# Attention's scores of two groups of heads, with products on different rows of TensorE's array next to each other in its queue

## The chip, the cores and the metric

The kernel runs on one core of a Trainium2 chip. The core has five engines, each with a queue of its own that it works through in order: TensorE (PE; its weight loads are shown as PEld) multiplies matrices into PSUM, VectorE (DVE), ScalarE (ACT) and GpSimdE (POOL) work element by element, and SyncE (SP) issues transfers. The metric is the time of one launch in microseconds (us), the median over several runs.

## The reference

One decoder layer with three parts, each followed by a residual add and a layer norm, for 4 batches of 512 tokens with 512 features:

- attention inside windows of 128 tokens. The input is compressed to 256 features; there are 16 heads of 16 features. Per window and head: `scores = q @ k.T * scale + rel_bias[rel]`, `probs = softmax(scores)`, `ctx = probs @ v`, and the output projection back to 512 features;
- a state-space recurrence (512 channels, 16 states each) over the context, gated with the attention's output;
- a feed-forward with ternary weights (the signs of W_g, W_u and W_d, 2048 hidden features) on activations rounded to 8 bits.

The bias `rel_bias[rel]` is the same 128x128 matrix for every head and window.

## The kernel before

The work is written as threads: generators that emit instructions and yield a cost. `weave` (L885) draws from them in the order of planned times and sets a priority; the framework's scheduler, which keeps a time line of its own, then fixes the order of each engine's queue. An edit in one thread can so move the instructions of all others. On the chip the queues run in order, and semaphores tie them together. The threads are, per batch: the recurrence's inputs, its steps, attention's projections (`attn_qk`, L574), four attention windows (`attn_window`, L603; a window waits for the one two before it), and the gate. After all windows comes the feed-forward: `ffn_load` gives attention's memory back and loads the signs of W_d (`ffn_setup2`, L738, the tile sd), and eight half batches follow (`ffn`, L750).

PSUM has eight banks. Four of them form one ring, from which `bank(...)` (L107, L110) draws for scores, projections and feed-forward; the others belong to the recurrence (`da`, `y`) and to its inputs and gates.

An attention window takes its 16 heads in four groups of four. The transposed q and k lie so that the four heads of group g stand in the 32 rows from 32g on, in NM = 2 blocks of features. `scores(g)` (L622) draws a bank and does on TensorE: two products with the identity that put the bias into the bank (high and low part, L625, 128x512), and two products q.k on the rows of the group (L634), each for two heads and 256 columns. k is kept in two versions, one for each half of the 32 rows, with the other half zero, so that one product gives two heads. A `tile_position` of (32g, 0) names the group's 32 rows of the array. VectorE then takes the maximum per head (L642). The loop over groups calls `scores(g + 1)` before it works on group g: four exponentials on ScalarE (L658), four transposes into the same bank (L662), a copy (L664), and four products with v (L669). The window ends with transposes, the output projection (L701) and the residual add (L702).

A recurrence step (`ssm_steps`, L357) has two or three large products on GpSimdE (L390, L400), four exponentials on ScalarE (L394), four scans on VectorE (L396), two products (L398), and four products on TensorE that sum the states into y (L404), with `tile_position` (0, 32j). There are 64 such steps, four for each batch and block of 128 channels, and each block has an opener (L380). The gate (`ssm_gate`, L415) multiplies y into the gate (L433), transposes it (L436) and adds it (L438). The feed-forward has products for the gate (L778), for the other factor (L802) and down (L830).

Of the kernel before, what the change touches and what calls it, by code (L numbers as in the profile page):

```python
# [15 lines left out]
ALU = mybir.AluOpType  # L16
AX = mybir.AxisListType

P = 128
# [6 lines left out]
NM = HC // P  # L26
# [41 lines left out]
HP = 1000  # L68
# [12 lines left out]
def decoder_layer_kernel(  # L81
# [21 lines left out]
    nc = tc.nc  # L103
# [6 lines left out]
    def bank(name):  # L110
        return psum.tile([P, 512], F32, tag="mm", name=name)
# [8 lines left out]
    ident = keep.tile([P, P], F32, tag="ident", name="ident")  # L120
# [98 lines left out]
    for j in range(NQ):  # L219
# [5 lines left out]
            lhsT=spreads[j],  # L225
            rhs=col[:, C_AL : C_AL + NE * DS],
            start=True,
            stop=True,
# [374 lines left out]
    def attn_window(b, w, aw, ap, aq, ws):  # L603
        n = f"{b}_{w}"
        tok = ts(w, P)
        cT, qT, kT = attn_x[b]
        xs = ap.tile([P, H], F32, tag="xa", name=f"xa{n}")
        nc.sync.dma_start(out=xs, in_=x[b * S + w * P : b * S + (w + 1) * P, :])
        yield 4

        v1 = ws["v1"][w % 2]
        pv = bank(f"v_ps{n}")
        for c in range(NM):
            nc.tensor.matmul(pv[:, :HC], lhsT=cT[:, c, tok], rhs=ws["v"][:, c, :], start=(c == 0), stop=False)
        nc.tensor.matmul(pv[:, :HC], lhsT=ws["one"], rhs=ws["row"][:, :HC], start=False, stop=True)
        nc.scalar.copy(v1[:, :, :DH], pv[:, :HC].rearrange("p (h d) -> p h d", d=DH))
        yield 1
        ntop = small.tile([P, HEADS], F32, tag="ntop", name=f"ntop_{n}", bufs=2)
        NG4 = HEADS // 4
        pscs = {}  # L620

        def scores(g):  # L622
            psc = bank(f"sc_ps{n}_{g}")
            for i in range(2):
                nc.tensor.matmul(  # L625
                    psc,
                    lhsT=ws["ident"],
                    rhs=ws["bias"][i].unsqueeze(1).to_broadcast([P, 4, P]),
                    start=(i == 0),
                    stop=False,  # L630
                )
            rows_ = ts(g, 32)
            for m in range(NM):
                nc.tensor.matmul(  # L634
                    psc[:, ts(m, 2 * P)],
                    lhsT=qT[rows_, m, tok],
                    rhs=kT[rows_, m, :, tok],
                    start=False,
                    stop=(m == NM - 1),
                    tile_position=(32 * g, 0),  # L640
                )
            nc.vector.tensor_reduce(  # L642
                ntop[:, 4 * g : 4 * g + 4], psc.rearrange("p (h k) -> p h k", k=P), AX.X, ALU.max, negate=True
            )
            pscs[g] = psc

        scores(0)
        yield 1
        pa = None
        for g in range(NG4):  # L650
            if g + 1 < NG4:
                scores(g + 1)
                yield 1.5
            psc = pscs.pop(g)
            sc = ap.tile([P, 4, P], F32, tag="sc", name=f"sc_{n}_{g}")
            for j in range(4):
                h = 4 * g + j
                nc.scalar.activation(sc[:, j, :], psc[:, ts(j, P)], AF.Exp, bias=ntop[:, h : h + 1])  # L658

            pt = psc  # L660
            for j in range(4):
                nc.tensor.transpose(pt[:, ts(j, P)], sc[:, j, :], ident)  # L662
            scT = ap.tile([P, 4, P], F32, tag="scT", name=f"scT_{n}_{g}")
            nc.scalar.copy(scT.rearrange("p h k -> p (h k)"), pt)  # L664
            if pa is None:

                pa = bank(f"a_ps{n}")
            for j in range(4):
                nc.tensor.matmul(  # L669
                    pa[32 * j : 32 * j + 32, ts(g, P)],  # L670
                    lhsT=v1[:, 4 * g + j, :],
                    rhs=scT[:, j, :],
                    start=True,
                    stop=True,
                    tile_position=(0, 32 * j),
                )
            yield 2
        av = ap.tile([P, NG4, P], F32, tag="scT", name=f"av_{n}")
        nc.scalar.copy(av.rearrange("p g q -> p (g q)"), pa)

        pq = pa
        for g in range(NG4):
            nc.tensor.transpose(pq[:, ts(g, P)], av[:, g, :], ident)
        pq3 = pq.rearrange("p (h d) -> p h d", d=32)
        den = small.tile([P, HEADS, 1], F32, tag="den", name=f"den_{n}", bufs=2)
        nc.vector.reciprocal(den, pq3[:, :, DH : DH + 1])
        at = ap.tile([P, HC], F32, tag="at", name=f"at_{n}")
        nc.vector.tensor_tensor(
            at.rearrange("p (h d) -> p h d", d=DH), pq3[:, :, :DH], den.to_broadcast([P, HEADS, DH]), ALU.mult
        )  # L690
        yield 3
        pt = pa
        for c in range(NM):
            nc.tensor.transpose(pt[:, ts(c, P)], at[:, ts(c, P)], ident)
        aT = ap.tile([P, HC], F32, tag="at", name=f"aT_{n}")
        nc.scalar.copy(aT, pt[:, :HC])
        yield 2
        po = pa
        nc.tensor.matmul(po, lhsT=ws["one"], rhs=ws["row"][:, HC:], start=True, stop=False)
        for c in range(NM):  # L700
            nc.tensor.matmul(po, lhsT=aT[:, ts(c, P)], rhs=ws["d"][:, c, :], start=False, stop=(c == NM - 1))  # L701
        nc.vector.tensor_tensor(xs, xs, po, ALU.add)  # L702
        nc.sync.dma_start(out=x0d[b][:, w, :], in_=xs)
# [216 lines left out]
    for b in range(B):  # L920
        threads.append((TP[b], after([], ssm_inputs(b), f"inputs{b}"), OP))
        threads.append((T0[b], after([f"inputs{b}"], ssm_steps(b, DT[b]), f"steps{b}"), OS))
        threads.append((TG[b], after(attn[b * NT : (b + 1) * NT] + [f"gate{b - 1}"] * (b > 0), ssm_gate(b), f"gate{b}"), OG))
        threads.append((TA[b] - AQ, after(["biases"], attn_qk(b, *aps), f"qk{b}"), OA))
        for w in range(NT):
            k = b * NT + w
            needs = [f"qk{b}"] + attn[k - 2 : k - 1] if k > 1 else [f"qk{b}"]
            threads.append((TA[b] + w * AW, after(needs, attn_window(b, w, *aps), attn[k]), OA))
# [68 lines left out]
```

## Time and profile before

| What | us |
|---|---|
| median of 9 runs | 831.48 (825.98 to 845.48) |
| the profiled execution's own time | 832.68 |
| its span, from the first instruction to the last | 830.9 |
| TensorE busy | 758.7 (91%) |
| VectorE busy | 649.0 (78%) |
| ScalarE busy | 591.8 (71%) |
| GpSimdE busy | 557.6 (67%) |
| score products q.k (L634), busy on TensorE | 74.1 |
| bias products (L625), busy on TensorE | 34.0 and 25.7 |
| attention's last residual add ends at | 539.3 |
| the recurrence's last y product starts at | 678.3 |
| starts of the down products of the eight half batches | 548.3, 585.4, 637.6, 678.8, 711.8, 742.4, 771.6, 800.8 |

How to read the profile: a row of the groups names the line, the engine, the operation, the tiles written and read, the form and the count, then the busy time in us and the mean duration in ns, and then the idle time before these instructions and who ended it. A product of 32-bit values has two passes, so that it shows as two records. The mean duration of a product contains the time that it takes to run through the array, which overlaps with the next one; what a product costs the queue is read from one start to the next. In the rows of 40 slices a digit is a tenth of the slice (20.8 us) in which the engine was busy. The chain is the work that ended last, followed back from the end.

### The profile page before, as it was taken

The page shows a single profiled execution, that of the slowest core. Times are in us where ns is not written, and L with a number is a line of the kernel's source. Part 1 is how long each engine was busy: PE and PEld are TensorE (multiplying, and loading weights), DVE is VectorE, ACT ScalarE, POOL GpSimd, SP SyncE. Part 2 cuts the span into 40 slices and gives each one's busy share as a digit, 9 for nine tenths or more (in the row PEclk, how much of TensorE's full clock was granted, in tenths as well). Part 3 has the DMA queues.
Part 4 walks back from the last instruction along what each step waited for, and adds up shares of the span by engine and source line. Part 5 has one row for each costly group of instructions (what it writes and reads, how often), then busy time and mean ns, then how long its engine had stood idle before and what let it go on. Part 6 is the DMA issues. An engine that isn't in the chain of part 4 may idle for free.

```text
span 830.9 us, 11702 instructions
## 1 busy us (share of the span) xinstructions
PE 758.7 (91%) x3906; PEld 413.0 (50%) x3906; DVE 649.0 (78%) x943; ACT 591.8 (71%) x1038; POOL 557.6 (67%) x323
## 2 busy tenths in 40 slices
PE   9977799999899999999988998889788999999995
PEld 4323244444344444434444454546464667777773
DVE  4459586899899986989988888989998978553542
ACT  3568889786866867786787878687596776845551
POOL 2158489599758968878876886797889944233342
PEclk9998898999989989899999999999999999999998
DMA  7887688866242536646153276582334112301100
GB/s 214 302 267 223 216 266 307 301 221 210 88 140 84 166 110 208 218 143 225 58 176 114 92 248 235 168 333 58 128 109 145 52 40 102 91 24 51 52 26 26
DMA packets 82784, 129.49 MB, mean 156 GB/s; under 512 B 18690, under 2 KB 29074, under 8 KB 81444
## 3 DMA queue, kind: packets, MB, share of 16 engines
q1 hardware_dynamic: 65844, 108.77, 40.2%
q10 hardware_dynamic: 16880, 19.98, 7.0%
q8 instruction: 31, 0.51, 0.3%
q14 instruction: 29, 0.24, 0.1%
HBM read 91.48 MB, written 37.23 MB: 155 GB/s over the span
## 4 chain that ended last, share of the span: by engine, by line
PE 55%; DVE 17%; ACT 12%; DMA 7%; issue 5%; POOL 2%; SPq 1%; ACTq 0%; DVEq 0%; POOLq 0%
PE d_ps L830 10%; PE y L404 6%; PE sc_ps L634 5%; DVE da L396 4%; PE u_ps L802 4%; PE g_ps L778 4%; DVE state L396 3%; PE a_ps L701 3%; PE sc_ps L625 3%; PE c_ps L568 2%; PE in_ps L273 2%; ACT da L394 2%; PE sc_ps L662 2%; DMA sgd<-sgn_sgd 2%; DVE state L398 2%
## 5 line engine op out<-in xcount | busy, mean ns | idle before, releaser
L390 POOL TENSOR_TENSOR state<-du,bc 128x1024 f32<-128x1024 f32 x128 | 302.0, 2374 | 115.4 <-PE y L404 69.6
L394 ACT ACTIVATE da<-d,a_neg 128x512 f32<-128x512 f32 x256 | 174.9, 696 | 63.7 <-DVE state L398 38.6
L400 POOL TENSOR_TENSOR state<-state,bc 128x1024 f32<-128x1024 f32 x64 | 151.9, 2373 | 38.9 <-DVE state L396 24.4
L396 DVE TENSOR_TENSOR_SCAN state<-da,state 128x512 f32<-128x512 f32 x128 | 152.5, 1208 | 31.5 <-ACT da L394 19.9
L396 DVE TENSOR_TENSOR_SCAN da<-da,state 128x512 f32<-128x512 f32 x128 | 152.9, 1214 | 16.3 <-ACT da L394 16.3
L823 POOL TENSOR_TENSOR lo<-gs,hi 128x512 fp32r<-128x512 f32 x64 | 82.5, 1293 | 103.4 <-ACT hi L821 87.9
L404 PE MATMUL y<-state,sel 128*32 128x512 f32 x512 | 104.0, 659 | 7.5 <-DVE state L398 4.6
L398 DVE TENSOR_TENSOR state<-da,bc 128x512 f32<-128x512 f32 x128 | 84.7, 678 | 0.8
L658 ACT ACTIVATE sc<-sc_ps,ntop 128x128 f32<-128x128 f32 x256 | 74.0, 375 | 11.2 <-DVE ntop L642 10.4
L821 ACT CAST hi<-gs 128x512 fp32r<-128x512 f32 x64 | 39.1, 615 | 56.4 <-DVE gs L811 42.8
L830 PE MATMUL d_ps<-sd,hi 128*128 128x512 f32 x256 | 73.8, 408 | 5.3 <-DVE gs L786 2.0
L830 PE MATMUL d_ps<-sd,lo 128*128 128x512 f32 x256 | 75.6, 417 | 0.0
L634 PE MATMUL sc_ps<-k,q 32*128 32x256 f32 x256 | 74.1, 410 | 0.7 <-ACT q L590 0.7
L802 PE MATMUL u_ps<-taken,su 128*128 128x256 bf16 x512 | 67.6, 273 | 6.5 <-DVE gs L811 4.2
L778 PE MATMUL g_ps<-taken,sg 128*128 128x256 bf16 x512 | 67.6, 276 | 4.5 <-DVE gs L811 3.2
L811 DVE TENSOR_TENSOR gs<-gs,u_ps 128x512 f32<-128x512 f32 x64 | 43.5, 680 | 34.6 <-PE u_ps L802 34.5
L786 DVE TENSOR_TENSOR gs<-g_ps,taken 128x512 f32<-128x512 f32 x64 | 43.4, 683 | 31.6 <-PE g_ps L778 28.1
L802 PEld LDWEIGHTS <-su 128*128 128x128 fp8e4 x512 | 46.3, 98 | 30.7 <-issue 23.5
L778 PEld LDWEIGHTS <-sg 128*128 128x128 fp8e4 x512 | 46.9, 98 | 28.0 <-issue 22.4
L634 PEld LDWEIGHTS sc_ps<-k,q 32*128 32x128 f32 x256 | 42.6, 187 | 30.0 <-issue 24.0
L830 PEld LDWEIGHTS d_ps<-sd,hi 128*128 128x128 f32 x256 | 45.1, 189 | 18.5 <-ACT hi L821 3.1
L642 DVE TENSOR_REDUCE ntop<-sc_ps 128x4 f32<-128x512 f32 x64 | 43.3, 677 | 13.8 <-PE sc_ps L634 13.6
(161 smaller groups left out, 1191.4 us busy)
## 6 DMA issues: line engine op xcount, KB each, us to landing
d<-dd SPq DMA_DIRECT2D x60, 256.0 KB, 3.8
du<-dud SPq DMA_DIRECT2D x60, 256.0 KB, 4.6
bc<-bcd SPq DMA_DIRECT2D x32, 256.0 KB, 4.0
xT<-in_xT_dram SPq DMA_DIRECT2D x16, 256.0 KB, 4.7
xa<-in_x_dram SPq DMA_DIRECT2D x16, 256.0 KB, 3.6
raw_sgd<-in_wgT_dram SPq DMA_DIRECT2D x16, 256.0 KB, 4.5
ud<-u ACTq DMA_DIRECT2D x4, 1024.0 KB, 4.3
uq<-ud SPq DMA_DIRECT2D x16, 256.0 KB, 3.0
```

The source lines that it names most:

```text
L390: nc.gpsimd.tensor_tensor(st, du, bb.unsqueeze(1).to_broadcast([P, 2, S]), ALU.mult)
L394: nc.scalar.activation(da, d[:, j, :], AF.Exp, scale=a_neg[:, a : a + 1])
L396: nc.vector.tensor_tensor_scan(to, da, st[:, j, :], 0.0, ALU.mult, ALU.add)
L398: nc.vector.tensor_tensor(st[:, j, :], da, cb, ALU.mult)
L400: nc.gpsimd.tensor_tensor(st, st, cb.unsqueeze(1).to_broadcast([P, 2, S]), ALU.mult)
L404: nc.tensor.matmul(y[ts(j, EB), :], lhsT=sel, rhs=sts[j], start=False, stop=(n == NG - 1), tile_position=(0, EB * j))
L634: nc.tensor.matmul(psc[:, ts(m, 2 * P)], lhsT=qT[rows_, m, tok], rhs=kT[rows_, m, :, tok], start=False, stop=(m == NM - 1), tile_position= ...
L658: nc.scalar.activation(sc[:, j, :], psc[:, ts(j, P)], AF.Exp, bias=ntop[:, h : h + 1])
L778: nc.tensor.matmul(pg[:, ts(j, HS)], lhsT=sg[:, c, ts(2 * f2 + j, P)], rhs=qT[:, c, :], start=(c == 0), stop=(c == NC - 1),)
L802: nc.tensor.matmul(pu[:, ts(j, HS)], lhsT=su[:, c, ts(2 * f2 + j, P)], rhs=qT[:, c, :], start=(c == 0), stop=(c == NC - 1),)
L823: nc.gpsimd.tensor_tensor(lo, g2, hi.bitcast(F32), ALU.subtract)
L830: nc.tensor.matmul(pos[t], lhsT=part[:, j, ts(t, P)], rhs=sd[:, 2 * f2 + j, :], start=(f2 + j == 0 and part is parts[0]), stop=(f2 == NF2 ...
```

## The change

`scores` takes two groups at once, (0, 1) and then (2, 3). It first draws the two banks and issues the four bias products, then the four products q.k in the order block 0 of both groups, block 1 of both groups. These four are held back until the last bias product has been scheduled (`issue_after`) and get a higher priority, so that they stand next to each other in the queue. The two maxima follow. The loop no longer asks for the scores of group g + 1 ahead of the work on group g: it asks for a pair before groups 0 and 2. The planned costs per window change from 1 and three times 1.5 to twice 2.

```diff
-        def scores(g):
-            psc = bank(f"sc_ps{n}_{g}")
-            for i in range(2):
-                nc.tensor.matmul(
-                    psc,
...
-            rows_ = ts(g, 32)
-            for m in range(NM):
-                nc.tensor.matmul(
-                    psc[:, ts(m, 2 * P)],
-                    lhsT=qT[rows_, m, tok],
-                    rhs=kT[rows_, m, :, tok],
...
+        def scores(gs):
+
+            for g in gs:
+                pscs[g] = bank(f"sc_ps{n}_{g}")
+                for i in range(2):
+                    last_bias = nc.tensor.matmul(
+                        pscs[g],
...
+            with tc.issue_after(last_bias.ins), tc.high_priority(HP):
+                for m in range(NM):
+                    for g in gs:
+                        nc.tensor.matmul(
+                            pscs[g][:, ts(m, 2 * P)],
+                            lhsT=qT[ts(g, 32), m, tok],
+                            rhs=kT[ts(g, 32), m, :, tok],
+                            start=False,
+                            stop=(m == NM - 1),
+                            tile_position=(32 * g, 0),
+                        )
...
-        scores(0)
-        yield 1
+
         pa = None
         for g in range(NG4):
-            if g + 1 < NG4:
-                scores(g + 1)
-                yield 1.5
+            if g % 2 == 0:
+                scores((g, g + 1))
+                yield 2
             psc = pscs.pop(g)
```

More of the change, by code (lines that the diff above doesn't have):

```diff
@@ L620, in attn_window @@
         pscs = {}
-        def scores(g):
-            psc = bank(f"sc_ps{n}_{g}")
-            for i in range(2):
-                nc.tensor.matmul(
-                    psc,
[L627 to L630, printed above, removed]
-                )
-            rows_ = ts(g, 32)
-            for m in range(NM):
-                nc.tensor.matmul(
-                    psc[:, ts(m, 2 * P)],
-                    lhsT=qT[rows_, m, tok],
-                    rhs=kT[rows_, m, :, tok],
[L638 to L645, printed above, removed]
@@ L647, in attn_window @@
-        scores(0)
-        yield 1
+        def scores(gs):
[4 more added lines that the diff above has]
+                        pscs[g],
+                        lhsT=ws["ident"],
+                        rhs=ws["bias"][i].unsqueeze(1).to_broadcast([P, 4, P]),
+                        start=(i == 0),
+                        stop=False,
+                    )
[9 more added lines that the diff above has]
+                            tile_position=(32 * g, 0),
+                        )
+            for g in gs:
+                nc.vector.tensor_reduce(
+                    ntop[:, 4 * g : 4 * g + 4], pscs[g].rearrange("p (h k) -> p h k", k=P), AX.X, ALU.max, negate=True
+                )
```

## The prediction

> **What bounds the kernel now.** I read the page first (engines, slices, chain, groups), then the trace in three places: TensorE's timeline around the attention scores, the busy time by stage, and the order of the instructions in the two builds. The page:
>
> ```profile
> PE 758.7 (91%) x3906; PEld 413.0 (50%) x3906; DVE 649.0 (78%) x943; ACT 591.8 (71%) x1038; POOL 557.6 (67%) x323
> ...
> PE   9977799999899999999988998889788999999995
> ...
> DVE  4459586899899986989988888989998978553542
> ...
> PE 55%; DVE 17%; ACT 12%; DMA 7%; issue 5%; POOL 2%; SPq 1%; ACTq 0%; DVEq 0%; POOLq 0%
> PE d_ps L830 10%; PE y L404 6%; PE sc_ps L634 5%; DVE da L396 4%; PE u_ps L802 4%; PE g_ps L778 4%; DVE state L396 3%; PE a_ps L701 3%; PE sc_ps L625 3%; PE c_ps L568 2%; PE in_ps L273 2%; ACT da L394 2%; PE sc_ps L662 2%; DMA sgd<-sgn_sgd 2%; DVE state L398 2%
> ...
> L634 PE MATMUL sc_ps<-k,q 32*128 32x256 f32 x256 | 74.1, 410 | 0.7 <-ACT q L590 0.7
> ```
>
> TensorE is the main bound, but from slice 9 to slice 32 VectorE is nearly as full. The products that the change pairs (L634) are 74.1 us of TensorE and about 5% of the chain, some 42 us. What one costs, and what two cost next to each other on different rows, stands in TensorE's timeline, since the scheduler put one such pair into the first window by itself:
>
> ```profile
> 63.11 0.69 PE L634 MATMUL sc_ps<-k,q 32*128 32x256 f32 x2
> 63.73 1.06 PE L404 MATMUL y<-state,sel 128*32 128x512 f32 x8
> 64.73 0.70 PE L634 MATMUL sc_ps<-k,q 32*128 32x256 f32 x4
> ...
> 142.92 1.13 PE L634 MATMUL sc_ps<-k,q 32*128 32x256 f32 x4
> 143.98 0.44 PE L694 MATMUL a_ps<-ident,at 128*128 128x128 f32 x2
> ```
>
> A product is two records (two passes). At 63.11 one product takes 0.69 us. At 64.73 two products of groups 0 and 1 take 0.70 us together. At 142.92 the two products of one group, on the same rows, take from 142.92 to 143.98, 1.06 us. So on the same rows they queue up, on different rows they run side by side. The stages, cut at 539.3 us, where the last residual add of attention (L702) ends and the feed-forward's second stage may start:
>
> ```profile
> core 0: us, PE busy (x) PEld busy (x) DVE busy (x) ACT busy (x) POOL busy (x), PEclk, DMA share, GB/s
> 120.00:539.30 419.30, 393.36 (x1958) 185.38 (x1957) 368.75 (x490) 324.41 (x653) 328.67 (x163) 0.95 0.54 177
> 560.00:640.00 80.00, 66.88 (x398) 43.38 (x395) 77.62 (x118) 58.47 (x80) 67.93 (x41) 0.98 0.35 111
> 539.30:830.90 291.60, 262.80 (x1624) 186.12 (x1623) 206.78 (x358) 187.34 (x244) 170.28 (x119) 0.98 0.26 89
> ```
>
> From 120 to 539.3 us TensorE is 94% busy and VectorE 88%; from 560 to 640 us, where TensorE has 13 us of idle time, VectorE reaches 97%. That is how dense VectorE gets when it is the bound.
>
> **The change, part by part.** No instruction is added or taken out; the counts of the two builds agree on every engine. What changes is order.
>
> *1. The products, side by side.* Today 64 groups x 1.06 us = 67.8 us. In the new order 31 of the 32 pairs stand as four products in a row, on rows of g and g+1 in turn. A block should take what one group takes plus what the pair at 64.73 took beyond one product, 0.01 us: 32 x 1.07 = 34.2 us. The difference is 33.6 us; less about 0.6 us for the pair that already overlaps, 33 us. Bounds: nothing, if they don't overlap; 33 us by the pair's row, and I take that, because it is the same form on the same engine. The biases' products (L625) keep their number and price.
>
> The Trainium skill has a lower price for this. TensorE: Matmul & The Clock Gate, Part 3, "Measured speedup vs the span model", tells of four row tiles that gave 3.07 times the speed, 77% of the ideal; an estimate from that for two tiles is 1.53 times, 23.6 us instead of 33.
>
> *2. The order, which the scheduler worked out anew.* Both scores of a pair now wait for the second bank, and the pair (2, 3) comes behind the work on groups 0 and 1 instead of one group ahead. The scheduler answers by letting the recurrence run ahead of attention. TensorE's last attention product of the last window stands behind 56 of the 64 recurrence steps, before behind 50; all 64 steps stand ahead of the last down products of the feed-forward's second half batch, before ahead of those of its third. Ahead of attention's last residual add VectorE gets: 22 scans x 1.21 us, 12 products x 0.68, 4 gate products x 1.23, 4 gate adds x 0.67, and 5 moments with their small steps, 5.5 us: 47 us more. TensorE gets 24 state products at 104.0/256 = 0.41 us, 2 openers at 17.3/16 = 1.08, 16 transposes at 11.1/64 = 0.17, less 16 gate products at 67.6/512 = 0.13: 13 us more. All of it is taken out behind that point, so it is moved and not added. SyncE's queue follows: the four loads of sd (L742) stand behind eight more issues, some 0.4 us each by these loads' own median of 417 ns, 3 us that go by beside the work ahead of attention's end.
>
> *3. When attention ends.* TensorE: (393.4 - 33 + 13) / 0.938 = 398 us, from 120 on: 518 us. VectorE: (368.75 + 47) / 0.97 = 429 us: 549 us. VectorE at today's 88%: 473 us: 593 us. So VectorE, not TensorE, is late next, and the end of attention comes somewhat later than today's 539, not earlier. I take 549, because with TensorE only 373/429 = 87% busy the stretch is like 560 to 640 us (TensorE 84%, VectorE 97%). The ends 518 and 593 stay for the range.
>
> *4. From there to the end.* TensorE's 262.8 us become 250, and 28.8 us were idle. Of these 13 lie in 560 to 640 us, where VectorE was full; VectorE has 47 us less to do there, and I let half of that idle time go: 250 + 22 = 272 us instead of 291.6.
>
> *Sum.* 549 + 272 = 821 us of span, against 830.9. The profiled execution took 832.68, 1.8 over its span and 1.2 over the median of 831.48, so the median should be 821 + 1.8 - 1.2, about 821. Of 33 us of TensorE time some 10 become time. The ends: 518 + 272 = 790; 593 + 272 = 865.
>
> On ScalarE and GpSimdE I cost the reordering at nothing: in 120 to 539.3 us they are 77% and 78% busy, and VectorE hides them. Were that cover gone, their next limit is GpSimdE, 7.1 us a step (three operations of 2.37) for six more steps, 43 us on 329: 372 of the 429 us, still under.
>
> The Trainium skill also has a rule that speaks against the change: TensorEngine Tiling (Array Packing), "PSUM Bottleneck", says that tiling speeds up TensorE and not the emptying of PSUM. The rows that bear on it are the 64 maxima of 0.68 us and 256 exponentials of 0.38 us, unchanged in number; by the rule alone attention would gain nothing and the time would stay at 831.
>
> **The rivals.**
>
> *All of it leaves (790 to 800).* If TensorE stays the bound throughout, 831.5 - 33 = 798. For it: 55% of the chain, and GpSimdE's wait for TensorE to give a state buffer back is 69.6 us over the span (the wait view: state L390 on y L404, 28 times), so a freer TensorE speeds the recurrence. Against: L634 is 42 us of the chain, of which half is 21; and VectorE at 88% has no room for more.
>
> *Nothing is left (831).* The recurrence moved ahead costs attention as much as the pairs give: attention ends at 559 instead of 549. For it: VectorE was never over 95% between 120 and 539 us in any stretch of 40 us.
>
> *Slower: the second bank (847).* There are four banks in the ring, and two windows, the projections and the feed-forward draw on it. A pair holds one bank while TensorE stands before the second bias product, and whatever is queued behind it stands too: the other window's transposes and the recurrence's y products, for which GpSimdE waits. If each of the 32 pairs waits for four exponentials of another group to end, 4 x 0.375 = 1.5 us, that is 48 - 33 = 15 us more. It decides from 33/32 = 1.03 us per pair on. For it: today a group asks for one bank at a time. Against: today the weight loads of L625's first half stood idle 24.6 us over 64 groups, of which only a part is a wait for a bank, under 0.4 us each; and the new order lets other work in between the two biases in most pairs. The group's row (busy us, mean ns, idle us before it and by whom):
>
> ```profile
> L625 PEld LDWEIGHTS sc_ps<-bias_hi,identr 128*128 128x128 f32 x64 | 12.3, 192 | 24.6 <-issue 7.3 <-ACT da L394 4.4 <-DVE xa L702 2.3
> ```
>
> *It doesn't do what it says (835).* The products don't overlap in a row of four, and only the order is changed: attention by TensorE ends at 120 + 406/0.938 = 553, and 272 to 285 us follow. The pair at 64.73 speaks against it.
>
> **How the numbers follow.** My case 0.42, with a range of its own of 808 to 827; all of it 0.12; nothing 0.15; the second bank, or VectorE kept at its old density by other waits, 0.28; no overlap 0.03. A measurement of this kernel can tell about 0.5%, 4.2 us. Faster by more than that: 0.42 + 0.12 = 0.54. Within it: 0.15 and a bit, 0.16. Slower: 0.30. For eight in ten I leave out the far end of the first rival and the part of the slower case above 852 (the end at 865 needs the old density throughout): 796 to 852.
>
> **What would show it.** Step 1: L634 busy at about 35 to 40 us instead of 74, in blocks of eight records of some 1.1 us. Step 2: the last residual add of attention behind more of the recurrence, and the recurrence's last y product well before 678 us. Step 3: that residual add ending near 549 us, with VectorE at 96 to 97% and TensorE at 87% from 120 us on. Step 4: some 272 us after it. I am wrong if L634 stays near 70 us; if idle time before the biases' products (L625) grows past 1 us per pair; or if VectorE stays at 88% in that stage, which would put the end past 850.

## The result, and the profile after

The changed kernel takes 882.5 us (median; 877.8 to 888.3) against 833.4 us for the kernel before in the same comparison: 1.062 times the time, 95% interval 1.060 to 1.065. The ratio is taken from fast launches alone: the kernel before has some slower ones at a lower clock (up to 863.5 us), which its median contains. Forecast were 821 us. The profiled execution has a span of 876.4 us.

The page of the changed kernel, in the lines that answer to those shown of before:

```profile
PE 745.3 (85%) x3906; PEld 401.7 (46%) x3906; DVE 650.7 (74%) x943; ACT 591.1 (67%) x1038; POOL 555.8 (63%) x323
...
PE   9966887769779897889959888687989999999995
...
DVE  5469574888888989889969989899888665544542
...
PE 34%; DVE 25%; ACT 19%; DMA 11%; issue 7%; SPq 2%; POOL 2%; ACTq 0%; DVEq 0%; POOLq 0%
PE d_ps L831 10%; DVE da L396 7%; DVE state L396 6%; PE u_ps L803 4%; ACT da L394 4%; PE g_ps L779 4%; DVE state L398 3%; ACT sc L659 3%; PE y L404 2%; DMA sgd<-sgn_sgd 2%; ACT L183 2%; DMA d<-dd 2%; PE c_ps L568 2%; PE in_ps L273 2%; DMA sdd<-raw_d 1%
```

The score products no longer stand among the costliest lines of the chain, and TensorE's share of it fell from 55% to 34%. VectorE and ScalarE have more of it (25 and 19%, before 17 and 12), but no engine is fuller than before: each has a smaller share of the span. The products did what was wanted. In TensorE's timeline (start, us, line and tiles) a block of four stands in a row, eight records, two for each product:

```profile
147.07 0.47 PE L627 MATMUL sc_ps<-bias_hi,identr 128*128 128x512 f32 x1
147.38 0.40 PE L627 MATMUL sc_ps<-bias_lo,identr 128*128 128x512 f32 x1
147.71 1.13 PE L637 MATMUL sc_ps<-k,q 32*128 32x256 f32 x8
148.77 1.98 PE L586 MATMUL q_ps<-cT,wq_s 128*128 128x512 f32 x4
152.67 0.44 PE L695 MATMUL a_ps<-ident,at 128*128 128x128 f32 x2 [1.91 <-DVE at L689]
156.67 2.15 PE L663 MATMUL sc_ps<-ident,sc 128*128 128x128 f32 x8 [3.56 <-ACT sc L659]
```

From 147.71 to 148.77 is 1.06 us for four products; before, two took that long. The last line shows a wait that is new: TensorE stands 3.56 us before the transposes, because the exponentials are not done. The groups of attention on TensorE (busy us, mean ns, then idle us before them and who ended the wait), before the change:

```profile
L662 PE MATMUL sc_ps<-ident,sc 128*128 128x128 f32 x256 | 42.8, 297 | 4.5 <-ACT sc L658 3.1 <-DVE state L398 1.3
L625 PE MATMUL sc_ps<-bias_hi,identr 128*128 128x512 f32 x64 | 34.0, 531 | 3.0 <-DVE xa L702 2.0 <-ACT v L616 0.7 <-ACT scT L664 0.3
```

and after it:

```profile
L663 PE MATMUL sc_ps<-ident,sc 128*128 128x128 f32 x256 | 48.9, 328 | 41.5 <-ACT sc L659 37.2 <-DVE at L689 3.2 <-DVE ntop L646 1.1
L637 PE MATMUL sc_ps<-k,q 32*128 32x256 f32 x256 | 38.9, 422 | 0.0
L627 PE MATMUL sc_ps<-bias_hi,identr 128*128 128x512 f32 x64 | 37.1, 579 | 9.1 <-ACT cT L571 4.7 <-ACT k L593 2.6 <-ACT v L616 1.6
```

The products cost 38.9 us instead of 74.1. The idle time before the transposes rose from 4.5 to 41.5 us, that before the biases' first products only from 3.0 to 9.1. By stage, cut at the end of attention's last residual add, which now comes at 601.5 us instead of 539.3:

```profile
120.00:601.50 481.50, 394.98 (x2028) 178.27 (x2028) 412.51 (x551) 349.14 (x691) 368.35 (x180) 0.89 0.50 166
601.50:876.40 274.90, 250.82 (x1564) 183.11 (x1564) 165.15 (x297) 163.28 (x209) 129.48 (x101) 0.96 0.23 76
```

The columns are those of the stages before: TensorE, weight loads, VectorE, ScalarE, GpSimdE, then the granted clock. From 120 us to attention's end TensorE is 82% busy and VectorE 86%: neither is full. The recurrence's y products, before and after (count, shortest, median and longest ns, first and last start in us):

```profile
L404 PE MATMUL y<-state,sel x512: 589/617/1062, 53.2 to 677.7; 128*32 128x512 f32 x171
```

```profile
L404 PE MATMUL y<-state,sel x512: 589/617/1063, 53.1 to 678.4; 128*32 128x512 f32 x171
```

The last one starts at 678.4 us, before at 677.7. The recurrence did not get faster by a microsecond; attention fell 62 us behind it, and 62 less what the rest got shorter (291.6 to 274.9) is the 45.5 us between the two spans.

### The profile page after: what moved, and what is told of

It is laid out like the page before. It is cut to its first block, busy times and chain, and to the rows that moved or that the text cites. A ratio compares the mean times of both kernels' runs of the same rounds, so it can differ in the third digit from the quotient of the medians.

```text
span 876.4 us, 11708 instructions
## 1 busy us (share of the span) xinstructions
PE 745.3 (85%) x3906; PEld 401.7 (46%) x3906; DVE 650.7 (74%) x943; ACT 591.1 (67%) x1038; POOL 555.8 (63%) x323
## 4 chain that ended last, share of the span: by engine, by line
PE 34%; DVE 25%; ACT 19%; DMA 11%; issue 7%; SPq 2%; POOL 2%; ACTq 0%; DVEq 0%; POOLq 0%
PE d_ps L831 10%; DVE da L396 7%; DVE state L396 6%; PE u_ps L803 4%; ACT da L394 4%; PE g_ps L779 4%; DVE state L398 3%; ACT sc L659 3%; PE y L404 2%; DMA sgd<-sgn_sgd 2%; ACT L183 2%; DMA d<-dd 2%; PE c_ps L568 2%; PE in_ps L273 2%; DMA sdd<-raw_d 1%
## 5 line engine op out<-in xcount | busy, mean ns | idle before, releaser
L400 POOL TENSOR_TENSOR state<-state,bc 128x1024 f32<-128x1024 f32 x64 | 151.1, 2361 | 86.0 <-DVE state L396 56.8
L404 PE MATMUL y<-state,sel 128*32 128x512 f32 x512 | 101.8, 681 | 14.4 <-DVE state L398 14.0
L663 PE MATMUL sc_ps<-ident,sc 128*128 128x128 f32 x256 | 48.9, 328 | 41.5 <-ACT sc L659 37.2
L659 ACT ACTIVATE sc<-sc_ps,ntop 128x128 f32<-128x128 f32 x256 | 71.5, 380 | 14.0 <-DVE ntop L646 12.7
L831 PE MATMUL d_ps<-sd,lo 128*128 128x512 f32 x256 | 75.3, 416 | 0.0
L663 PEld LDWEIGHTS sc_ps<-ident,sc 128*128 128x128 f32 x256 | 33.3, 163 | 76.3 <-ACT sc L659 63.9
L831 PEld LDWEIGHTS d_ps<-sd,lo 128*128 128x128 f32 x256 | 45.3, 193 | 11.2 <-issue 2.5
```

The costliest lines, as they stand in the source:

```text
L400: nc.gpsimd.tensor_tensor(st, st, cb.unsqueeze(1).to_broadcast([P, 2, S]), ALU.mult)
L404: nc.tensor.matmul(y[ts(j, EB), :], lhsT=sel, rhs=sts[j], start=False, stop=(n == NG - 1), tile_position=(0, EB * j))
L831: nc.tensor.matmul(pos[t], lhsT=part[:, j, ts(t, P)], rhs=sd[:, 2 * f2 + j, :], start=(f2 + j == 0 and part is parts[0]), stop=(f2 == NF2 ...
```

## The experiments

The theories, as the expectations name them. A: the maxima, exponentials and transposes of a pair come as one lump with no scores ahead to fill the queue. B: TensorE stands before the second bank. C: the hold and the raised priority force an order on the scheduler. D, formed from the first four experiments: attention's place in the queue behind the recurrence sets its end, because the recurrence keeps its pace; the pair's demand for banks is what puts it there. "Steps" are the recurrence's steps that stand ahead of attention's last product in TensorE's queue, the output projection of the last window: 50 before the change, 56 after it.

**The products of a pair not alternating.**

```diff
-                for m in range(NM):
-                    for g in gs:
+                for g in gs:
+                    for m in range(NM):
```

> The changed kernel, but the four products of a pair in the order block 0 and 1 of group g, then block 0 and 1 of group g+1, so that only the middle two stand on different rows; all else as changed (875 to 888 us on record: 882.5). Theory A (the pair's maxima, exponentials and transposes come as one lump with no scores ahead to fill the queue; the overlap itself is good but lies beside other waits): 882 to 900 us, with the products' busy time back near 60 to 74 us and TensorE's wait before the transposes as long as in the changed kernel, about 40 us. Theory B (TensorE stands before the second bank): the same 882 to 900. Theory C (the order that the held-back, prioritised products force on the scheduler): the same. If the overlap of products itself does harm, below 870 us.

Measured: 875.9 us (1.057, 1.051 to 1.062), below the 882 to 900 of A, B and C. As an experiment on the overlap it failed, and in an instructive way: the products overlap all the same, at 41.4 us busy. The order of the rows in the queue doesn't matter to this. TensorE's timeline of this run:

```profile
146.28 1.14 PE L637 MATMUL sc_ps<-k,q 32*128 32x256 f32 x8
147.35 0.66 PE L684 MATMUL a_ps<-ident,av 128*128 128x128 f32 x4
```

Four products in 1.07 us, though two of the same rows stand one behind the other.

**No hold and no priority.**

```diff
-            with tc.issue_after(last_bias.ins), tc.high_priority(HP):
+            with ExitStack():
```

> The changed kernel without the hold and the raised priority for the four products: the pair still draws two banks together and is still asked for before groups 0 and 2. The scheduler then puts the two products of a group next to each other in nearly all cases, so there is no overlap, and the last window ends behind 51 of 64 recurrence steps, as before (50), not 56. Theory C (the forced order): 825 to 845 us. Theory A (lump, no scores ahead): 860 to 885 us, since the scores of groups 2 and 3 still come behind the work on groups 0 and 1 in the program. Theory B (second bank): 870 to 900 us.

Measured: 856.0 us (1.032, 1.024 to 1.039), between the numbers of C and of A. Attention ends at 553 us, with products at 75.3 us and hence no overlap. So the hold, less what the overlap gave back, cost some 26 us, and about half of the loss is left without it.

**Both pairs ahead of any work on a group.**

```diff
-            if g % 2 == 0:
-                scores((g, g + 1))
+            if g == 0:
+                scores((0, 1))
+                yield 2
+                scores((2, 3))
                 yield 2
```

> The changed kernel, but both pairs of a window are asked for ahead of any work on a group, so that scores again run ahead; a window then wants all four banks of the ring. Overlap kept (31 rows of four). The last window ends behind 53 steps. Theory A: 835 to 860 us, with TensorE's wait before the transposes at half or less of the changed kernel's 41 us. Theory B: 885 us or more, idle time before the biases' products over 30 us. Theory C: between before and after, 845 to 870 us, by the 53 steps.

Measured: 853.8 us (1.029, 1.025 to 1.034), inside the forecasts of A and of C; attention ends at 561 us, TensorE's idle time before the transposes is 17.6 us, that before the biases 5.0. B falls: a window asks for all four banks, and TensorE doesn't stand before them.

**The second pair ahead of group 1.**

```diff
-            if g % 2 == 0:
-                scores((g, g + 1))
+            if g < 2:
+                scores((2 * g, 2 * g + 1))
```

> The changed kernel, but the second pair of a window is asked for ahead of the work on group 1 and not behind it. Overlap kept. The last window ends behind 57 steps. Theory A: 845 to 865 us, TensorE's wait before the transposes 15 to 30 us. Theory B: 882 us or more, since three banks are held at once. Theory C: 882 us or more, since the recurrence runs as far ahead as in the changed kernel.

Measured: 895.6 us (1.081, 1.076 to 1.085), against A, and as B and C had it; for B the wait before the biases' first products, 17.4 us, is small. The scores run ahead and it got worse; attention ends at 621 us. The wait before the transposes, 34.2 us, is shorter than in the changed kernel, and the time longer: that wait isn't what sets the time. What does agree with all of these runs is the place of attention (57, 51, 53 and 57 steps). So theory D was formed, and the next runs change the place by means that have nothing to do with pairs.

**The kernel before, with three banks in the ring.**

```diff
-    psum = ctx.enter_context(tc.tile_pool(name="psum", bufs=8 - BDA - BY - BX, space=bass.MemoryType.PSUM))
+    psum = ctx.enter_context(tc.tile_pool(name="psum", bufs=7 - BDA - BY - BX, space=bass.MemoryType.PSUM))
```

> The kernel before with a ring of three banks instead of four; no pairing, scores one group ahead. In its queue the last window ends behind 63 of 64 recurrence steps (50 with four banks). Theory D (a pair's two banks make the ring too short, so the planned order lets attention fall behind the recurrence; the recurrence keeps its pace of 9 to 10 us a step, and attention ends when the step ahead of it ends): attention's end near 660 to 680 us, the time 920 to 960 us. Theory A (lump of a pair's exponentials): 830 to 850 us, because nothing is paired.

Measured: 943.7 us (1.135, 1.129 to 1.142), inside D's forecast; attention ends at 657.3 us, just short of D's 660 to 680. The residual adds of attention (count, shortest, median and longest ns, first and last start):

```profile
L702 DVE TENSOR_TENSOR xa<-xa,a_ps x16: 652/677/687, 132.1 to 656.6; 128x512 f32<-128x512 f32 x16
```

and TensorE's group of the biases in the same run:

```profile
L625 PE MATMUL sc_ps<-bias_hi,identr 128*128 128x512 f32 x64 | 38.7, 604 | 7.3 <-ACT scT L664 5.1 <-ACT v L616 1.8 <-ACT q L590 0.3
```

Attention ends 118 us later than with four banks, and all that TensorE waits before these products is 7.3 us. The missing bank isn't paid there as a wait but as an order: with three banks the scheduler puts 63 steps ahead of attention's last product instead of 50.

**The kernel before, with attention's start planned later.**

```diff
-TA = (10, 45, 95, 135)
+TA = (20, 80, 170, 250)
```

> The kernel before with only the planned start times of attention's batches set later (20, 80, 170, 250 instead of 10, 45, 95, 135); banks, groups and products as before. The last window ends behind 59.5 steps. Theory D, its second half (the place in the order against the recurrence sets attention's end, whatever the reason): attention ends at 625 to 650 us, the time 885 to 920 us. Theory A or a cost that lies in the pair itself: 830 to 850 us.

Measured: 895.1 us (1.077, 1.071 to 1.083), inside D's forecast; attention ends at 640.8 us. Nothing in the program but four planned times was changed here, and it costs more than the pairs do.

**The v product in another bank, in both kernels.**

```diff
-        pv = bank(f"v_ps{n}")
+        pv = ssm_bank(f"v_ps{n}")
```

> The changed kernel, but a window's v product is put into the bank of the recurrence's inputs and gates, so that the ring of four serves scores, context and the rest alone. 31 pairs in rows of four as in the changed kernel; the last window ends behind 48 steps. Theory D: attention ends at 505 to 535 us and the time is 795 to 830 us. Theory A: the pair is the same lump and no scores run ahead, so 850 to 880 us with TensorE's wait before the transposes at 30 to 45 us.

> The control for the run above: the kernel before with the same move of the v product to the other bank. The last window ends behind 48 steps. Theory D: attention ends at 505 to 530 us, the time 810 to 830 us; the difference to the run above is what the overlap of products is worth once the banks are the same: 0 to 25 us in favour of the pairs. Theory A: 815 to 830 us, and 30 to 50 us better than the pairs.

Measured: 926.3 us (1.115, 1.110 to 1.120) with pairs and 891.8 us (1.073, 1.069 to 1.077) without. Both times missed both theories' forecasts: the bank that I gave away belongs to the recurrence's inputs, and the recurrence now stands still at the turn of a batch (61 and 72 us between two steps with pairs, 50 us without, where the kernel before takes 9 and 13); its last y product starts at 778 and 736 us. Attention, behind 48 steps in both, ends at 566.6 and 564.7 us, some 50 us later than the place and the usual pace would have it. The pairs are 34 us slower here, which is the difference that A named; most of it lies behind attention's end (357 against 325 us). The shortage was moved, not taken away, and this pair of runs doesn't tell what the overlap is worth.

**No overlap in the same order.** Every group's products stand on the rows of group 0; the queues are the same as in the changed kernel.

```diff
-                            lhsT=qT[ts(g, 32), m, tok],
-                            rhs=kT[ts(g, 32), m, :, tok],
+                            lhsT=qT[ts(0, 32), m, tok],
+                            rhs=kT[ts(0, 32), m, :, tok],
...
-                            tile_position=(32 * g, 0),
+                            tile_position=(0, 0),
```

> The changed kernel with every group's products on the rows of group 0, so that they cannot run side by side (the scores of groups 1 to 3 are therefore those of group 0; the amount of work is the same). The order of all five queues is the same as in the changed kernel, instruction for instruction, so this measures the overlap by itself. Products' busy time back from 39 to 70 to 80 us. If TensorE's time is on the path in this stage: 905 to 916 us (882 and some 25 to 33). Theory D, where the path runs through the recurrence's pace and the waits for maxima and exponentials: 882 to 897 us.

Measured: 898.2 us (1.076, 1.063 to 1.089), just over D's forecast and under the other. The products' group on TensorE in this run:

```profile
L637 PE MATMUL sc_ps<-k,q 32*128 32x256 f32 x256 | 71.4, 422 | 0.0
```

So the overlap saves 32.5 us of TensorE's time (71.4 to 38.9), and by the ratios (1.076 to 1.062) some 11 us of the kernel's time, by the two spans (895.1 to 876.4) 19 us. The four launches of this run took 886.3 to 901.6 us and the intervals of the two ratios overlap a little, so the gain is likely but not clear of noise. Without the overlap the change costs 7.6%, some 63 us.

**Attention further ahead, with pairs.** Both pairs first, and a window waits for the one three before it.

```diff
-            needs = [f"qk{b}"] + attn[k - 2 : k - 1] if k > 1 else [f"qk{b}"]
+            needs = [f"qk{b}"] + attn[k - 3 : k - 2] if k > 2 else [f"qk{b}"]
```

> Both pairs asked for ahead of any work on a group, and a window waits for the one three before it instead of two, so that the plan lets attention run further ahead. Overlap in 31 rows of four. The last window ends behind 49 steps. Theory D: attention ends at 525 to 545 us, the time 812 to 840 us. Theory A (the lump of eight or sixteen exponentials at once costs, wherever the window stands): 845 to 860 us, as with both pairs first (854).

Measured: 844.3 us (1.016, 1.008 to 1.024). Attention ends at 534.8 us, inside D's forecast, but the rest takes 306 us instead of 292, so that the time lies just above D's and just below A's.

**Both pairs first, without the hold** (the edit of the second run, on the third).

> Both pairs asked for ahead of any work on a group, without the hold and the priority: hardly any overlap, the last window ends behind 49 steps. Theory D: attention ends at 530 to 550 us, the time 825 to 845 us. Theory A: 845 to 870 us.

Measured: 851.0 us (1.022, 1.013 to 1.031); attention ends at 541 us, inside D's forecast, and the time above it, again by a longer rest (310 us). The time lies in A's forecast, but of A's wait little is left: TensorE stands 4.4 us before the transposes, as in the kernel before (4.5).

**Both pairs first, and the recurrence's steps at a lower priority.**

```diff
-OX, OP, OS, OG, OA, OF = 0, -90, 0, 0, -30, 40
+OX, OP, OS, OG, OA, OF = 0, -90, 80, 0, -30, 40
```

> Both pairs asked for ahead of any work on a group, with the hold, and the recurrence's steps at a lower priority (offset 80 instead of 0). Overlap in 31 rows of four, the last window ends behind 50 steps instead of 53. Theory D: attention ends at 530 to 550 us, the time 820 to 842 us, against 854 with 53 steps. Theory A: unchanged, 850 to 858 us.

Measured: 850.5 us (1.023, 1.014 to 1.033). Attention's end is as D has it, 536 us, the time is not, and lies in A's forecast: 312 us of rest follow, and the recurrence's last y product starts at 693 us instead of 678. An earlier end of attention bought nothing here.

**The last batch's inputs earlier, on the 844 us kernel; and the same without overlap.**

```diff
-TP = (-45, 50, 100, 170)
+TP = (-45, 50, 100, 150)
```

> Both pairs first and windows three apart (844 us), and the inputs of the recurrence's last batch planned earlier (150 instead of 170): their last projection of dt stands behind 44 steps, as before the change (44.5), not behind 47. The last window ends behind 51 steps. In the 844 us run the recurrence stood still between its 48th and 52nd step (69 us for four steps, 39 before the change). Theory D: attention ends at 545 to 560 us, the rest shrinks from 306 to 275 to 285 us, the time is 822 to 838 us. If the rest lay in something else: 842 us or more.

> The run above with all products on the rows of group 0 (the scores of groups 1 to 3 are those of group 0): the same order of all five queues, no overlap. It prices the overlap where attention is not held back. If the overlap's TensorE time is on the path there: 18 to 33 us more than the run above. If not: 0 to 10 us.

> As the first of these runs, with the last batch's inputs planned at 130: their last projection of dt stands behind 42 steps, attention's last window behind 52. Theory D: within 8 us of the first of these runs, on either side, attention's end 10 us later and the rest shorter by as much.

Measured: 840.0 us (1.010, 1.007 to 1.013) at 150 and 840.3 us (1.009, 1.005 to 1.012) at 130; 847.9 us (1.018, 1.013 to 1.023) without overlap. The recurrence does get to its 52nd step earlier (540 us instead of 558), yet in the run at 150 attention ends at 534 us, before D's 545 to 560, and 302 us follow, not 275 to 285: D missed both, and the time by 2 us. The run at 130 went as forecast: attention ends 9 us later and the rest is 7 us shorter. In this order the overlap is worth 8 us, inside the forecast for TensorE's time not being on the path (0 to 10): by the products' groups, 37.7 against 65.7 us, TensorE gets 28 us back and the kernel 8.

**The kernel before without running ahead.** Single groups, one bank at a time, and the scores of a group are asked for right before the work on it.

```diff
-        scores(0)
-        yield 1
         pa = None
         for g in range(NG4):
-            if g + 1 < NG4:
-                scores(g + 1)
-                yield 1.5
+            scores(g)
+            yield 1.4
```

> The kernel before with single groups, no pairs and no hold, but without running ahead: the scores of a group are asked for right before the work on that group. It needs fewer banks than the kernel before. The last window ends behind 58 of 64 steps. In the twelve kernels so far that keep the ring of banks to itself, attention ended 10.3 to 10.8 us times that number of steps, plus 4 to 13 us. By that rule: attention's end at 605 to 635 us and the time at 870 to 900 us. If only the pair's two banks and the lump were the trouble: 830 to 845 us.

Measured: 886.6 us (1.069, 1.061 to 1.077), as the rule of place and pace has it, and not 830 to 845. Attention ends at 616.1 us. The residual adds in the kernel before, in this run and in the changed kernel:

```profile
L702 DVE TENSOR_TENSOR xa<-xa,a_ps x16: 653/672/689, 137.8 to 538.7; 128x512 f32<-128x512 f32 x16
```

```profile
L699 DVE TENSOR_TENSOR xa<-xa,a_ps x16: 654/672/689, 141.2 to 615.4; 128x512 f32<-128x512 f32 x16
```

```profile
L703 DVE TENSOR_TENSOR xa<-xa,a_ps x16: 659/674/689, 136.9 to 600.8; 128x512 f32<-128x512 f32 x16
```

This takes away from the kernel before only that scores run one group ahead, and costs as much as the whole change does. TensorE's idle time before the transposes is 18.0 us here and 41.5 us in the changed kernel, with the two kernels' times 4 us apart; the lump of theory A is a sign of the loss and not its size. It also leaves the first half of D, the pair's demand for banks, not shown: this kernel wants fewer banks than the kernel before and falls back to 58 steps, and both pairs first wants all four and falls back to 53 only.

The rule in numbers, from the profiled executions (the steps are those ahead of attention's last product in TensorE's queue, the third column is when TensorE ended the last of them):

| kernel | steps | us at that step | us per step | attention ends | span |
|---|---|---|---|---|---|
| before | 50 | 526.8 | 10.5 | 539.3 | 830.9 |
| changed | 56 | 589.6 | 10.5 | 601.5 | 876.4 |
| changed, no overlap | 56 | 606.5 | 10.8 | 617.7 | 895.1 |
| both pairs first | 53 | 552.4 | 10.4 | 560.7 | 851.6 |
| both pairs first, windows three apart | 49 | 522.5 | 10.7 | 534.8 | 840.4 |
| before, not running ahead | 58 | 603.8 | 10.4 | 616.1 | 883.5 |
| before, attention planned later | 59.5 | 635.8 | 10.7 | 640.8 | 892.2 |
| before, three banks | 63 | 649.3 | 10.3 | 657.3 | 940.5 |

The other runs that keep the ring to itself have 10.2 to 10.8 us per step, and attention ends 4 to 14 us after its step; the two with the v product in the other bank have 11.1 and 11.4 us. A pace that varies by 5% is some 30 us at 56 steps.

## Why the prediction was wrong

**Part 1 was right.** Forecast were blocks of 1.07 us and 35 to 40 us in all; measured were 1.06 us and 38.9 us. The 33 us of TensorE time are there (32.5 us by the run without overlap). The lower price, my estimate of 23.6 us from the figure for four tiles in the Trainium skill, TensorE: Matmul & The Clock Gate, Part 3, "Measured speedup vs the span model", is contradicted: two tiles run at 1.9 times the speed here, 74.1 to 38.9, not at 1.53; four tiles were not measured. But TensorE's busy time over the span fell by only 13.4 us, because its other groups, the same in number, rose from 684.6 to 706.4 us, the transposes (42.8 to 48.9) most. From 120 us to attention's end TensorE is busy 395 us, forecast 373.

**Part 2 was right in the place and wrong in what it means.** Attention's last residual add does stand behind 56 steps and behind more of VectorE's work, forecast as 47 us (the terms add up to 48): VectorE is busy 412.5 us from 120 us to attention's end, forecast 416. But I read "the recurrence runs ahead" as the recurrence getting faster, and wrote that its last y product would come well before 678 us. It came at 678. And the lost running ahead, which this part names, got no price in the sum.

**Part 3, "When attention ends", is the step that failed.** I took VectorE's density for the bound, 97% as in a stretch where TensorE has time to spare, and so 549 us; its upper end, at today's 88%, was 593. Measured were 601.5 us at 86%: 481.5 us from 120 us on instead of 429. No engine was full. Attention's end follows its place: in every kernel of the table attention ends 5 to 13 us after the step that stands ahead of it, and that step comes at 10.3 to 10.8 us times its number. Before the change 50 x 10.5 + 12 = 537 us, after it 56 x 10.5 + 12 = 600 us: the profile of before and the two orders, which I had, would have given 600 us, had I taken the pace as fixed. VectorE's share tells much the same, because the place also says how much of VectorE's work comes first: in all the runs that keep the ring it is 83 to 88% from 120 us to attention's end, never 97, so that my own upper end, 593, was 8 us off. These runs can't separate a fixed pace from a fixed share of VectorE; both rule out the 97%.

A belief that helped the failure, and stands in my first rival, was that a freer TensorE speeds the recurrence, since GpSimdE waited 69.6 us for state buffers that y products gave back. The wait did shrink, and another grew. GpSimdE's waits (us in total, times, longest) before and after the change:

```profile
POOL state L390 <- PE y L404: 69.6, 28, 9.5
...
POOL state L400 <- DVE state L396: 24.4, 14, 4.7
```

```profile
POOL state L400 <- DVE state L396: 56.8, 24, 8.2
...
POOL state L390 <- PE y L404: 27.0, 19, 4.6
```

27.0 us on TensorE instead of 69.6, but 56.8 on VectorE's scans instead of 24.4. What holds the pace at about 10.5 us a step, over engines none of which is full, no run here takes apart; it stays open.

**Part 4 was right in its sum.** Forecast were 272 us from attention's end to the end of the span, 250 of them busy; measured were 274.9 and 250.8. That some 6 us of idle time would go was a guess, and no run tests its reason. Together with 601.5 it gives the span of 876.4, so nearly the whole miss is part 3: 601.5 - 549 = 52.5 us, and 2.9 us here.

**The rivals.** "Slower" got 0.30, and the range ended at 852. The end at 865, which needed today's density throughout, was named and left out of the range; it was the nearest number. The mechanism that I gave for it was wrong: TensorE doesn't stand before the second bank (9.1 us before the biases' first products, 32 pairs, under 0.3 us each). The other half of that rival, VectorE at its old density, and the third sign of being wrong, 88% in that stage and an end past 850, are what came. The lost running ahead acts through the order that the scheduler plans, and the waits show less than its price (18.0 us before the transposes for 52 us of time). That a pair's second bank acts so too is not shown. What the parts contribute: taking the running ahead away from the kernel before costs 52 us by itself (886.6 against 834.1 us); giving it back to the changed kernel, with the hold kept, leaves 854; dropping the hold instead leaves 856. The two are not additive and the runs don't split them further.

**What I weighed wrongly.** TensorE's 55% of the chain and the 42 us of L634 in it made me look for time in the products. The overlap is worth 8 us in one order and, by the ratios or the spans, 11 to 19 in the other. And the rule of the Trainium skill that spoke against the change, TensorEngine Tiling (Array Packing), "PSUM Bottleneck", was of no use as I applied it (no gain, 831): the maxima and exponentials kept their number and were not the bound. The same page's "Gotcha 1: PSUM Pressure" says that row tiling increases the pressure on PSUM, since different row tiles write to different banks. No run here prices a pair's second bank by itself; the run with three banks shows what a bank less costs a kernel without pairs, 112 us.

A version that beats the kernel before was not found. The best with overlap takes 840 us, in which attention ends at 534 us, 5 us earlier than before, and 302 us follow instead of 292. By the starts of its down products the loss lies between the third and the fourth half batch (49 us apart, before 41), where TensorE is idle 11.5 us and before 0.7; what makes it wait there is open.

## What to carry to other kernels

Where a scheduler lays several chains into in-order queues, look first at where the change puts one chain relative to the other, count what stands ahead of it, and multiply by the pace that the profile of before shows. Here that gives attention's end to within some 20 us in every order that left the recurrence its banks, and an engine sum with a density taken from another stretch missed it by 52 us; it doesn't give what follows attention's end. An edit that saves work on the busiest engine but makes a stage ask for its inputs later, or leaves it a buffer less, can be paid for in that order, and the waits need not show the price. Before pairing work to overlap it, see whether the stage still runs ahead of its consumer afterwards.

## What the runs showed of the hardware that was not expected

Products on different 32-row groups overlap without standing alternately in the queue, an exception to queues that run in order: in the order group g twice, then group g+1 twice, four products take 1.07 us, as they do alternating (1.06 us). Their eight records start at 0, 14, 320, 334, 536, 549, 752 and 765 ns after the first (alternating: 0, 7, 320, 327, 536, 543, 752 and 759), so a product on free rows must have gone ahead of one that waited for its own. The records don't name the group, so this rests on the order in which the products were written, on the starts and on the total.

TensorE's granted clock is lower in the changed kernel: 0.89 instead of 0.95 from 120 us to attention's end, where TensorE is 82% busy instead of 94%, and 0.917 instead of 0.954 over the span. The busy share alone doesn't tell the clock: in the same stage the 840 us kernel has 0.93 with TensorE 85% busy, and the changed kernel without overlap 0.86 with 88%. A part of the lost time may be a slower TensorE. An estimate of its bound: TensorE's products outside the scores took 21.8 us longer in all (684.6 to 706.4), so that this can explain at most about half of the 45.5 us between the spans; how much it does was not measured.
